# Every third early adapter weight in a place of its own, and two places for a low-rank table

## The chip, the cores and the metric

The kernel runs on one core of one Trainium2 chip. The metric is device time in microseconds (us) of one launch, taken as the median of several runs on the chip. Beside the runs there is one profiled execution, which gives a trace of every instruction with its engine, its start, its length and what it waited for. The engines are TensorE (PE; its weight loads are shown apart as PEld), VectorE (DVE), ScalarE (ACT), GpSimd (POOL) and SyncE (SP). SP computes nothing here; it issues most of the transfers from memory.

## The reference

The input x has 32 samples of 64 rows (H) and 1,024 columns (L), in float32. Four layers each add their output to x:

```python
x = x + L0(x, log_dt, C, log_A_real, A_imag, D, lengths)  # long convolution along L
x = x + einsum('bsi,boi->bso', x, W1[ids1])               # adapter weights, chosen per sample
x = x + einsum('bij,bkj->bik', x, W2[ids2])               # the same with a second set
x = x + gated_ffn(x)                                      # with low-rank parts chosen by ids3
```

Layer 0 builds a kernel of length 1,024 for each of the 64 rows from complex exponentials and convolves each row with it. Layers 1 and 2 multiply each sample (64 x 1024) by a 1024 x 1024 matrix that an index of that sample chooses among 16. Layer 3 is silu(gate) * up, followed by down, with a hidden size of 2,752, and each of gate, up and down has a low-rank part of rank 16, which is chosen per sample too:

```python
t = einsum('bri,bni->bnr', A[ids3], x)
base + einsum('bor,bnr->bno', B[ids3], t) * 0.5
```

## The kernel before, in words

The samples are cut into four chunks (c = 0 to 3) of eight samples, 512 rows in all. The kernel first does the convolution for all 32 samples, then the adapters of chunk 0 alone, and then the gated layers chunk by chunk. The adapters of chunk c + 1 are woven into the gated layers of chunk c, where there is other matmul work around them.

**Adapter weights.** `layers(c)` (line 136) gives the order of the adapters of one chunk: layer 0 of one sample, then layer 1 of the sample before it, and so on, sixteen in all. One adapter's matrix is loaded as eight tiles of 128 x 1024 numbers (KT = 8, 512 KB each); in this document one such tile is a weight. Chunk 0 has 16 x 8 = 128 of them, and they are numbered here in the order of use, from 0. For each weight `adapter` (line 234) does eight matmuls, which the trace shows as sixteen records each, on four column strips side by side, into the PSUM tile pa. After the eighth weight DVE transposes pa into y (L251) and adds y to x (L253). A second layer's adapter waits for the x of its own sample; between the two lies another sample's adapter.

**Places for weights.** `wpool` (line 98) is a ring of nine tiles, named wa in the trace when weights use it. It is shared with all later weights (wf, wr, wd) and with the tiles cv that bring the convolution's results. A tile of the ring is free for a new load when the matmuls that read its last content are done. `early` (lines 125 to 129) is a list of twenty more places: sixteen tiles of a pool `epool` that is closed after the adapters of chunk 0, and four quarters (x_early) of the x tile that later holds chunk 1. They are used once each.

**Order of loads.** The generator `weights` (line 145) issues the loads in the order of use, each with `nc.sync.dma_start` on SP (L161). For each adapter it first reads the matrix index from ids_sb into a register of SP (L151). The line `wt = early.pop(0) if early else wpool.tile(...)` gives the first twenty weights the single-use places and every later one the next tile of the ring. `fetch` (line 171) is called once by each of the sixteen steps of the convolution (`convolve`, line 861), between the load of its input uf (L865) and the loads of its kernels hk (L873): eight weights at the first step and one at each other, 23 in all, kept in the list `ahead`. The rest are issued from `adapter` as the program comes to them. SP works through its instructions in order: a load whose place is not free holds up everything behind it.

**The order on the engines.** The program's text sets the order on TensorE. On the other engines a scheduler of the language sets it, and `tc.issue_after` keeps it from moving an instruction ahead of a given one. The list `loads` holds the last load of each adapter; a read of an index is not moved ahead of the load four adapters back, and the loads of chunk 1's x, of cv and of wd_rest (L188, L193, L549) are not moved ahead of `loads[2 * BC - 1]`, the last weight of chunk 0.

**The low-rank tables.** `b_rows` (line 274) gathers on POOL, with an indirect transfer (L267), the rows of the B tables of gate and up that belong to the samples of the chunk, into a tile bgu of 128 x 4 x 128 numbers (256 KB). It is called once for the part left over (`rest`, m = 10) and for m = 0 to 9 (`gated`). bgu has one buffer (`bufs=1`). `expand` (line 345) multiplies it with tm_g and tm_u into four PSUM tiles pe (L353), which ACT copies to lt (L363). POOL also issues, in its own order, the A tables raw_g, raw_u and raw_d (L297, eight transfers each time) and the gathers into wl (L267); the indices for all gathers come from il, which SP loads (L210) and DVE turns into rowf, rows_half and rows (L212 to L219).

**From the adapters to the gated layers of chunk 0.** After the last weight TensorE does the low-rank products pl_g and pl_u, then `rest`: two pr groups (L470), pe_rest, a third pr group; then the first `gated`: pe from bgu, and seven groups pf (L409) each for gate and up.

Of the kernel before, what the change touches and what calls it, by code (L numbers as in the profile page):

```python
# [8 lines left out]
F32 = mybir.dt.float32  # L9
# [4 lines left out]
SP = mybir.EngineType.SP  # L14
POOL = mybir.EngineType.Pool

P = 128
B, H, L = 32, 64, 1024
NS = 64
KT = L // P  # L20
NCK = 4
BC = B // NCK
# [6 lines left out]
MB = FM // 2  # L29
EARLY = 16  # L30
FIRST_LOADS = 8
PLACES = EARLY + 4 + 9
HA = 4
SEG = 3
TH = TC // 2
# [3 lines left out]
NE = 16  # L39
# [30 lines left out]
def kernel(  # L70
# [23 lines left out]
    nc = tc.nc  # L94

    cpool = ctx.enter_context(tc.tile_pool(name="cpool", bufs=1))
    xpool = ctx.enter_context(tc.tile_pool(name="xpool", bufs=2))
    wpool = ctx.enter_context(tc.tile_pool(name="wpool", bufs=9))
    psum = ctx.enter_context(
        tc.tile_pool(name="psum", bufs=8, space=bass.MemoryType.PSUM)  # L100
    )
# [5 lines left out]
    def ps_tile(name):  # L107
        return psum.tile([P, 512], F32, tag="ps", name=name)
# [8 lines left out]
    def x_tile(c):  # L117
        return xpool.tile([P, KT, TC], F32, tag="x", name=f"x{c}")
# [6 lines left out]
    early = [epool.tile([P, L], F32, tag=f"e{i}", name=f"early{i}") for i in range(EARLY)]  # L125
# [6 lines left out]
    ids_sb = cpool.tile([1, 3 * B], I32, tag="ids", name="ids_sb")  # L132
    nc.sync.dma_start(ids_sb, ids)
    loads = []

    def layers(c):


        for b in range(c * BC, (c + 1) * BC + 1):
            if b < (c + 1) * BC:  # L140
                yield 0, b
            if b > c * BC:
                yield 1, b - 1

    def weights():
        for layer, b in (at_ for c in range(NCK) for at_ in layers(c)):
            with ExitStack() as after:
                if len(loads) > 3:

                    after.enter_context(tc.issue_after(loads[-4]))  # L150
                e = nc.values_load(  # L151
                    ids_sb[0:1, layer * B + b : layer * B + b + 1],
                    engines=[SP],
                    min_val=0,
                    max_val=NE - 1,
                )
            for kt in range(KT):
                name = f"wa{layer}_{b}_{kt}"
                wt = early.pop(0) if early else wpool.tile([P, L], F32, tag="w", name=name)
                w = (w1, w2)[layer]  # L160
                load = nc.sync.dma_start(  # L161
                    wt, w[bass.ds(e, 1), kt].rearrange("e p f -> p (e f)")
                )
                if kt == KT - 1:
                    loads.append(load.ins)
                yield wt

    stream = weights()
    ahead = []

    def fetch(ha):


        for _ in range(FIRST_LOADS if ha == 0 else 1):
            if len(ahead) < PLACES:
                ahead.append(next(stream))

    convolution(tc, cst, consts, xt, xf, ssm, lens, xs[0], cd, ps_tile, fetch)

    came = {}  # L180
    last_add = []

    def bring(c, quarters):

        if quarters[0] == 0:
            xs.append(x_tile(c))
            with tc.issue_after(loads[2 * BC - 1]):
                nc.sync.dma_start(xs[c], xt[:, c])  # L188
        n = H // HA // 4
        for q in quarters:  # L190
            t = wpool.tile([P, n * HA, KT * BC], F32, tag="w", name=f"cv{c}_{q}")
            with tc.issue_after(loads[2 * BC - 1]):
                nc.sync.dma_start(  # L193
                    t.rearrange("p i k -> p (i k)"),
                    cd[c - 1, :, q * n : (q + 1) * n].rearrange("p g e -> p (g e)"),
                )
            came[q] = t
# [36 lines left out]
    def adapter(layer, b):  # L234
        c, lo = b // BC, (b % BC) * H
        acc = ps_tile(f"pa{layer}_{b}")
        for kt in range(KT):
            wt = ahead.pop(0) if ahead else next(stream)
            for s in range(2):
                for i in range(4):  # L240
                    nc.tensor.matmul(  # L241
                        acc[i * S : (i + 1) * S, s * 256 : (s + 1) * 256],
                        xs[c][:, kt, lo + s * S : lo + (s + 1) * S],
                        wt[:, i * 256 : (i + 1) * 256],

                        start=(kt == 0 and s == 0),
                        stop=(kt == KT - 1),
                        skip_group_check=True,
                    )
        y = ypool.tile([P, 512], F32, tag="y", name=f"y{layer}_{b}")  # L250
        nc.vector.transpose(y, acc)  # L251
        cols = xs[c][:, :, lo : lo + H].rearrange("p k (s t) -> p k s t", t=S)
        nc.vector.tensor_add(cols, cols, y.rearrange("p (s k t) -> p k s t", s=2, t=S))  # L253

    def adapters(c):
        for layer, b in layers(c):
            yield adapter(layer, b)

    for _ in adapters(0):
        pass  # L260
    first.close()

    hpool = ctx.enter_context(tc.tile_pool(name="hpool", bufs=1, reuse_waits="tile"))
    gpool = ctx.enter_context(tc.tile_pool(name="gpool", bufs=2, reuse_waits="tile"))

    def gather(t, table, at_):
        nc.gpsimd.indirect_dma_start(  # L267
            out=t,
            out_offset=None,
            in_=table,  # L270
            in_offset=bass.IndirectOffsetOnAxis(ap=at_, axis=0),
        )

    def b_rows(c, piece):
        t = gpool.tile([P, 4, P], F32, tag="bgu", name=f"bgu_{c}_{piece}", bufs=1)
        gather(t.rearrange("p g f -> p (g f)"), bgu, rows[:, c, piece : piece + 1])
        return t

# [115 lines left out]
    def gated(c, m, xb, between):  # L394

        lt = expand(b_rows(c, m), f"{c}_{m}", (("g", 0), ("g", 1), ("u", 2), ("u", 3)))
        lt = lt.rearrange("p (g i) t -> p g i t", g=2)
        cs = []
# [51 lines left out]
    def rest(c):  # L450


        bt = b_rows(c, FM)
        for i in range(3):
            wt = wpool.tile([P, KT, P], F32, tag="w", name=f"wr{i}_{c}")
# [51 lines left out]
    def ffn(c, xb, others):  # L507
# [12 lines left out]
        def between(i):  # L520

            if i < STEPS:
                if c + 1 < NCK:
                    if i in (2, 4):
                        take(c + 1, (i - 2, i - 1))
                    if i in (0, 2):
                        bring(c + 1, (i, i + 1))
            else:
                other(AT_GATED)
# [3 lines left out]
        for block, (m0, m1) in enumerate(BLOCKS):  # L533
            last = m1 == FM
# [6 lines left out]
            if last:  # L541


                wl = gpool.tile([P, 2, 2, L // 2], F32, tag="wl", name=f"wl_{c}", bufs=1)
                for t in (0, 1):
                    wl_t = wl[:, t].rearrange("p i f -> p (i f)")
                    gather(wl_t[FIRST], bd, rows_half[FIRST, c, t : t + 1])
                    with tc.issue_after(loads[2 * BC - 1]):
                        nc.sync.dma_start(wl_t[SECOND], wd_rest)  # L549
                nc.vector.tensor_sub(wl[:, 1, 0], wl[:, 1, 0], wl[:, 1, 1])  # L550
            else:
                ins += [rest1, rest2.rearrange("p i t -> p (i t)")]
# [7 lines left out]
            for h in range(KH):  # L560
                name = f"{c}_{block}_{h}"
# [8 lines left out]
                for s0 in range(m0, m1, SEG):  # L570
# [4 lines left out]
                    at_ = s0 + block  # L575
                    wt = []
                    for i in (0, 1):
                        t = wpool.tile([P, 2, KH, P], F32, tag="w", name=f"wd{i}_{name}_{s0}")
# [4 lines left out]
                    if more:  # L583
                        w = [t[:, 0, nt] for t in wt]
# [3 lines left out]
                    elif end:  # L588
                        w = [[wl[:, t, i, h * P : (h + 1) * P] for i in (0, 1)] for t in (0, 1)]
                        tails = {1: (w[0][0], 0), 3: (w[0][1], 0), 4: (w[1][1], 1), 2: (w[1][0], 1)}  # L590
                    ws = stationary(wt, nt, f"{name}_{s0}")
                    for j in (0, 5, 6, 4, 1, 3, 2):
                        if end and j in tails:
                            w, t = tails[j]
# [44 lines left out]
    for c in range(NCK):  # L639
        xb = ffn(c, xb, adapters(c + 1) if c + 1 < NCK else iter(()))  # L640
# [444 lines left out]
```

## Time and profile before

| what | value |
|---|---|
| median of three runs | 2396.56 us (2396.1 to 2402.57) |
| time of the profiled execution | 2398.25 us |
| span of its trace | 2396.6 us |
| mean granted TensorE clock | 0.998 |
| TensorE busy | 2321.4 us, 97% |
| DVE, ACT, POOL busy | 1098.6, 309.7, 190.2 us |
| convolution on TensorE | to about 193 us |
| adapters of chunk 0 on TensorE | 193.1 to 349.7 us |
| first gated layer's pe | 383.39 us |
| bytes moved | 505.41 MB, mean 211 GB/s |

In the profile's rows of forty slices each digit is the busy share of a slice of about 60 us in tenths, 9 meaning 90% or more. A row of the timeline gives the start and the length in us, the engine, the line, the operation, the tiles (out<-in), the shape and the count of instructions merged into the row, and in brackets the idle time before it with what ended it. A row of waits gives who waited for whom, then the total in us, the number of times and the longest. "SPq" is SP's transfer queue. The clock is the share of full speed that TensorE was granted. The DMA share is the mean busy share of the core's 16 DMA engines.

### The profile page before, as it was taken

What the parts mean: (1) busy time and instruction counts of PE and PEld (TensorE: products, weight loads), DVE (VectorE), ACT (ScalarE), POOL (GpSimd) and SP (SyncE); (2) the same over time, 40 slices, a digit from 0 to 9 for tenths busy, and PEclk for the clock granted to TensorE, in tenths of its full rate; (3) what the DMA queues carried; (4) which work ended last, traced back from release to release, by engine and by line L of the source; (5) the groups of instructions that cost most, each with busy time, mean ns of one, the idle gap of its engine ahead of it and who ended that gap; (6) DMA issues with size and microseconds to landing.
All of it is one profiled execution on the core that took longest, in us unless ns stands there. A gap on an engine that the chain in (4) does not pass through costs nothing. (4 is left out here: it accounts for less than half of the span.)

```text
span 2396.6 us, 46124 instructions
## 1 busy us (share of the span) xinstructions
PE 2321.4 (97%) x19154; PEld 1838.7 (77%) x19154; DVE 1098.6 (46%) x2078; ACT 309.7 (13%) x605; POOL 190.2 (8%) x275
## 2 busy tenths in 40 slices
PE   5999889999999999999999999999999999999999
PEld 5995336877778787877777787777787787888888
DVE  7411124644354534643354544643354544554653
ACT  4200002110011101110011101110011101210210
POOL 4322001000000020000000020000000020000000
PEclk9999999999999999999999999999999999999999
DMA  8997994576666744576666644576666653223311
GB/s 304 367 335 283 408 409 126 185 260 209 237 247 228 245 148 154 185 264 216 240 251 215 241 155 154 180 265 215 242 252 215 239 159 113 82 84 108 100 56 62
DMA packets 165987, 505.41 MB, mean 211 GB/s; under 512 B 20354, under 2 KB 54402, under 8 KB 165266
## 3 DMA queue, kind: packets, MB, share of 16 engines
q1 hardware_dynamic: 147874, 463.87, 55.0%
q0 software_dynamic: 11104, 29.93, 3.8%
q10 hardware_dynamic: 6800, 8.65, 1.0%
q8 instruction: 151, 2.47, 0.4%
q14 instruction: 58, 0.48, 0.1%
HBM read 487.41 MB, written 14.97 MB: 210 GB/s over the span
## 5 line engine op out<-in xcount | busy, mean ns | idle before, releaser
L409 PE MATMUL pf<-xd,wf 128*128 128x256 f32 x2560 | 608.2, 382 | 0.0
L409 PEld LDWEIGHTS pf<-xd,wf 128*128 128x128 f32 x2560 | 482.9, 190 | 74.8 <-issue 6.4
L241 PE MATMUL pa<-wa,x 128*32 128x256 f32 x7872 | 454.9, 381 | 24.5 <-DMA wa<-in_w 21.9
L409 PE MATMUL pf<-xd,s 128*128 128x256 f32 x1920 | 454.0, 379 | 3.9 <-DVE c L430 3.3
L241 PEld LDWEIGHTS pa<-wa,x 128*32 128x32 f32 x7872 | 241.9, 110 | 230.1 <-DMA wa<-in_w 60.8
L409 PEld LDWEIGHTS pf<-xd,s 128*128 128x128 f32 x1920 | 364.6, 190 | 55.0 <-DVE c L430 4.5
L886 PE MATMUL pc<-uf,hk 128*128 128x256 f32 (+7 forms) x1024 | 153.8, 312 | 9.9 <-DMA hk<-kp 6.3
L601 PE MATMUL po<-act,wd 128*128 128x256 f32 x640 | 161.7, 383 | 0.0
L886 PEld LDWEIGHTS pc<-uf,hk 128*128 128x128 f32 x1024 | 148.6, 194 | 14.5 <-issue 8.8
L601 PE MATMUL po<-actd,wd 128*128 128x256 f32 x640 | 159.0, 379 | 0.0
L601 PE MATMUL po<-actd,s 128*128 128x256 f32 x640 | 159.0, 379 | 0.0
L267 POOL DMA_INDIRECT bgu<-in_bgu,rows x44 | 46.0, 1045 | 1363.2 <-PE pe L353 1292.6
L434 DVE TENSOR_TENSOR c<-pf,u 128x256 f32<-128x256 f32 x80 | 34.0, 425 | 235.5 <-PE pf L409 235.5
L601 PEld LDWEIGHTS po<-act,wd 128*128 128x128 f32 x640 | 119.5, 190 | 22.9 <-issue 6.3
L601 PEld LDWEIGHTS po<-actd,wd 128*128 128x128 f32 x640 | 121.6, 190 | 16.5
L601 PEld LDWEIGHTS po<-actd,s 128*128 128x128 f32 x640 | 121.6, 190 | 16.5
L363 ACT COPY lt<-pe 128x512 f32<-128x512 f32 x160 | 82.2, 600 | 341.1 <-PE pe L353 254.6
L251 DVE STREAM_TRANSPOSE y<-pa 128x512 f32<-128x512 f32 x64 | 45.5, 710 | 134.1 <-PE pa L241 134.1
L438 DVE TENSOR_TENSOR c<-c,lt 128x1024 f32<-128x1024 f32 x80 | 97.9, 1224 | 5.1
L381 DVE TENSOR_TENSOR s<-wf 128x512 f32<-128x512 f32 x80 | 54.9, 687 | 86.1 <-DMA wf<-in_wg 46.3
L381 DVE TENSOR_TENSOR s<-wd 128x384 f32<-128x384 f32 x64 | 31.2, 488 | 134.9 <-PE po L601 86.8
L470 PE MATMUL pr<-x,wr 128*128 128x512 f32 x192 | 84.2, 595 | 0.0
(169 smaller groups left out, 1828.0 us busy)
## 6 DMA issues: line engine op xcount, KB each, us to landing
wa<-in_w SPq DMA_DIRECT2D x492, 512.0 KB, 7.5
wf<-in_wg SPq DMA_DIRECT2D x80, 512.0 KB, 4.1
wf<-in_wu SPq DMA_DIRECT2D x80, 512.0 KB, 3.8
wd<-in_wd SPq DMA_DIRECT2D x96, 384.0 KB, 4.7
hk<-kp SPq DMA_DIRECT2D x30, 1024.0 KB, 8.3
x<-in_xt SPq DMA_DIRECT2D x4, 2048.0 KB, 11.1
uf<-in_xf SPq DMA_DIRECT2D x16, 512.0 KB, 5.1
early<-in_w SPq DMA_DIRECT2D x16, 512.0 KB, 8.5
```

The lines of the kernel that those rows point to most:

```text
L241: nc.tensor.matmul(acc[i * S : (i + 1) * S, s * 256 : (s + 1) * 256], xs[c][:, kt, lo + s * S : lo + (s + 1) * S], wt[:, i * 256 : (i + 1) ...
L251: nc.vector.transpose(y, acc)
L267: nc.gpsimd.indirect_dma_start(out=t, out_offset=None, in_=table, in_offset=bass.IndirectOffsetOnAxis(ap=at_, axis=0),)
L363: nc.scalar.copy(lt[:, :n, 2 * H * j : 2 * H * (j + 1)], ps[:, : n * 2 * H].rearrange("p (i t) -> p i t", i=n),)
L381: nc.vector.tensor_add(s1, a21, a22)
L409: nc.tensor.matmul(ps, ws[j][:, kt, :], xb[j][:, kt, :], start=start and kt == 0, stop=kt == KH - 1, skip_group_check=True,)
L434: nc.vector.tensor_add(cq[:, 1], pb, u)
L438: done = nc.vector.tensor_add(cf, cf, lt[:, g].rearrange("p i t -> p (i t)"))
L470: nc.tensor.matmul(ps, wt[:, kt, :], xs[c][:, kt, :], start=(kt == 0), stop=(kt == KT - 1),)
L601: nc.tensor.matmul(pss[j], ws[j][:, i, :], ab[m - m0][j], start=(m == m0 and home[j] % 2 == 0), stop=(m == m1 - 1), skip_group_check=True,)
L886: nc.tensor.matmul(ps[:, j, d * B :], hk[:, j, d * P : (d + 1) * P], uf[:, i + j, : KT - d, :].rearrange("p k b -> p (k b)"), start=(d == ...
```

## The change

The first 60 weights are now shared out between the two kinds of place by their number. Every third one (2, 5, 8, ..., 59) has one of the twenty single-use places, and the other forty go through the ring of nine. A new generator `first_weights` issues what can be issued without any wait, in the order of use: the nine first rotating weights (0, 1, 3, 4, 6, 7, 9, 10, 12) and all twenty with an own place, 29 in all. `fetch` draws from it, and what is left is issued right after the convolution. `weights` then hands out the weights in the order of use: those that are held already, and the others with a load at that point. The index of a matrix is read once for the part of an adapter that is issued early and once more for the part that is issued later. `done_first` takes the place of `loads[2 * BC - 1]`; both are the last load of chunk 0.

Apart from that, bgu takes the pool's own number of buffers, which is two.

```diff
+    def load_weight(e, layer, b, kt, own):
+        name = f"wa{layer}_{b}_{kt}"
+        wt = early.pop(0) if own else wpool.tile([P, L], F32, tag="w", name=name)
+        w = (w1, w2)[layer]
+        load = nc.sync.dma_start(wt, w[bass.ds(e, 1), kt].rearrange("e p f -> p (e f)"))
+        return wt, load.ins
+
+    own = {3 * i + 2 for i in range(len(early))}
+    held = {}
+
+    def first_weights():
+        rotating = [k for k in range(3 * len(early)) if k not in own][:ROTATING]
+        last, at_ = [], None
+        for k in sorted([*own, *rotating]):
+            layer, b = list(layers(0))[k // KT]
+            if at_ != k // KT:
+                at_, e = k // KT, adapter_id(layer, b, last)
+                last.append(None)
+            held[k], last[-1] = load_weight(e, layer, b, k % KT, k in own)
+            yield
+
     def weights():
+        k = 0
         for layer, b in (at_ for c in range(NCK) for at_ in layers(c)):
...
             for kt in range(KT):
-                wt = early.pop(0) if early else wpool.tile([P, L], F32, tag="w", name=name)
...
+                if k in held:
+                    yield held.pop(k)
+                else:
+                    if e is None:
+                        e = adapter_id(layer, b, loads)
+                        loads.append(None)
+                    wt, loads[-1] = load_weight(e, layer, b, kt, False)
+                    yield wt
+                k += 1
...
         for _ in range(FIRST_LOADS if ha == 0 else 1):
-            if len(ahead) < PLACES:
-                ahead.append(next(stream))
+            next(before, None)

     convolution(tc, cst, consts, xt, xf, ssm, lens, xs[0], cd, ps_tile, fetch)
+    for _ in before:
+        pass
...
-            wt = ahead.pop(0) if ahead else next(stream)
+            wt = next(stream)
...
-        t = gpool.tile([P, 4, P], F32, tag="bgu", name=f"bgu_{c}_{piece}", bufs=1)
+        t = gpool.tile([P, 4, P], F32, tag="bgu", name=f"bgu_{c}_{piece}")
```

## The prediction

> **What bounds the kernel now.** I read the page's slices first, then one-stretch tables, the waits of SP's DMA queue, and the timeline of TensorE at the two places that the diff touches.
>
> ```profile
> PE   5999889999999999999999999999999999999999
> DMA  8997994576666744576666644576666653223311
> ```
>
> TensorE fills every slice from the eighth on, so time can only be won or lost in the first 400 us, where its 75 us of idle time (2396.6 - 2321.4) nearly all lie: 28 us in the first 60 us, a few in the convolution, some 23 between 215 and 350, 5 at 378. Later it waits about 4 us. The stretches of the first adapters (columns: stretch, length, then busy us and count of PE, PEld, DVE, ACT, POOL; then clock, DMA share, GB/s):
>
> ```profile
> 195.00:200.00 5.00, 5.00 (x96) 3.03 (x100) 0.00 (x0) 0.00 (x0) 4.17 (x8) 1.00 0.37 121
> 200.00:205.00 5.00, 5.00 (x100) 3.01 (x96) 1.41 (x2) 0.00 (x0) 2.00 (x4) 1.00 0.23 70
> 205.00:210.00 5.00, 5.00 (x100) 2.99 (x92) 1.41 (x2) 1.05 (x1) 2.99 (x4) 1.00 0.21 62
> 225.00:349.00 124.00, 101.00 (x1512) 40.39 (x1516) 15.50 (x22) 1.99 (x2) 0.00 (x0) 1.00 1.03 408
> ```
>
> From 195 to 212 TensorE is full and the DMA engines are nearly idle; from 225 to 349 it is the reverse: transfers at 408 GB/s, TensorE waiting for each weight. The stage is bound by transfers, and it wastes 17 us of them at its start. The SP queue (210 us window from 200; columns: total, times, longest us) says why:
>
> ```profile
> SPq L161 <- PE pa L241: 28.1, 9, 25.8
> ```
>
> One wait of 25.8 us: the 30th load stands at SP until TensorE has used the 21st weight, since the first twenty lie in places that are used once. TensorE's timeline (start, us, instructions, count, idle before):
>
> ```profile
> 208.31 3.64 PE L241 MATMUL pa<-x_early,x 128*32 128x256 f32 x64
> 211.76 10.62 PE L241 MATMUL pa<-wa,x 128*32 128x256 f32 x192
> 223.24 1.07 PE L241 MATMUL pa<-wa,x 128*32 128x256 f32 x16 [0.86 <-DVE y L251]
> 225.72 2.18 PE L241 MATMUL pa<-wa,x 128*32 128x256 f32 x32 [1.42 <-DMA wa<-in_w]
> ```
>
> A weight is 16 records; 192 in 10.62 us is 0.885 us a weight when none is waited for. Weight 33 (from 0) starts at 225.72 and the last ends at 349.69: 95 weights at 1.305 us, the price by transfer. The issue of the first rotating load after the gap is at 212.87.
>
> The second place is at 378:
>
> ```profile
> 378.35 1.19 POOL L267 DMA_INDIRECT bgu<-in_bgu,rows  x1 [2.87 <-issue]
> 383.39 1.24 PE L353 MATMUL pe<-tm_g,bgu 32*128 32x128 f32 x16 [4.96 <-DMA bgu<-in_bgu,rows]
> 385.41 3.77 PE L409 MATMUL pf<-xd,wf 128*128 128x256 f32 x8
> ```
>
> TensorE stands 4.96 us for a gather that POOL issued behind sixteen raw_d loads, and then runs slowly: eight pf matmuls take 3.77 us, where the same eight take 1.89 at 402.8. The clock over this stretch:
>
> ```profile
> 384.00:386.00 2.00, 2.00 (x30) 1.68 (x27) 0.71 (x2) 0.53 (x2) 0.16 (x1) 0.50 0.00 0
> 386.00:388.00 2.00, 2.00 (x6) 1.64 (x5) 0.00 (x0) 1.52 (x4) 0.82 (x1) 0.50 0.13 27
> 390.00:392.00 2.00, 2.00 (x11) 1.77 (x10) 0.43 (x1) 0.37 (x1) 0.00 (x0) 1.00 0.00 0
> ```
>
> Half clock until about 389.
>
> **What the Trainium skill says.** "TensorE: Matmul & The Clock Gate", part 1, says that an idle window of about 3.4 us halves TensorE's clock and that as long a busy stretch restores it. The trace agrees for the 4.96 us gap (about 5.5 us at half), and is harsher once: after a 1.99 us gap at 131 the clock was 0.50 from 133.2 to 136; gaps of 1.50 and 1.42 us cost nothing. "DMA: Bandwidth & Descriptors", section "Anatomy of one DMA", gives a fixed 2.0 us plus bytes over 436 GB/s, 3.2 us for 512 KB; the quickest weight here landed 3.3 us after issue. The same page, "Issuing engines are not separate DMA queues": POOL's and SP's transfers share the 16 engines. The trace agrees: at 215 to 220 raw_u and weights together moved only 294 GB/s at a share of 0.92.
>
> **Part 1, the places.** Every third of weights 0 to 59 gets one of the twenty single-use places; weights 0, 1, 3, 4, 6, 7, 9, 10, 12 fill the ring of nine. As before 29 weights are loaded ahead, 23 of them inside the convolution and six behind it, none waiting for TensorE. Bytes and matmuls are the same; only which place a weight lies in changes.
>
> Weight 13 now needs the place of weight 0, which TensorE has used at about 195.6, so its load issues at about 195.8 and not at 212.87: 17.1 us of transfer time gained. What comes off:
> - The idle DMA time was not quite empty. POOL's raw_g, bgu and wl gathers and the last cd write ran in it: 0.37, 0.23 and 0.21 of three 5 us stretches, 4.05 us, less weights that were still arriving at 195. They now share the engines with weights. With the second bgu table (256 KB, about 0.65 us at 408 GB/s) I take 4.4 us; bounds 3.1 (1.25 MB at 408 GB/s) and 6.5 (small packets twice as dear, as raw_u's were: the first 33 weights came 4.4 us later than 1.305 us each and a 3.5 us landing give).
> - Pacing. While own places last, three weights on TensorE (2.66 us) free two places (2.61 us of transfer): balanced. 31 loads lose 31 x 0.02, 0.7 us.
>
> Net 17.1 - 4.4 - 0.7 = 12.0 us. From the other end: 195.8 + 3.5 + 98 x 1.305 + 1.07 (last weight) + 4.4 (raw_u, as before) + 4.4 + 0.7 = 337.8, against 349.7; the same sum without the two new terms from 212.87 gives 349.7, as measured. After 350 the work is TensorE's, so an earlier start comes off the end.
>
> The lead of nine rotating places is about 12 us of TensorE's work, and a lone landing takes 3.5, so TensorE has no reason to stop in weights 0 to 59.
>
> **Queues.** In the built order SP has three more reads of ids inside the convolution (0.27 + 0.15 + 0.02 us each; the interval from uf to the weight's issue is 1.15 us with one and 0.55 without). They stand ahead of the hk loads, for which TensorE waits there already (gaps of 0.32, 1.50, 1.99). Bounds: 0 if SP waits for a place anyway, 1.8 if all shows; a longer gap may add a half clock of 1.6. I take 0.8. Behind the convolution il's load moves behind six weights: I estimate that it lands before 195; on DVE rowf and rows then stand ahead of the first y transpose, needed at 201.65, 6 us of cover. Without that cover the second layer's first adapter would come late by the excess.
> On POOL the first wl gather moves behind raw_u, and both wl gathers now wait for TensorE's use of weight 17 (early5, about 211); their reader on DVE is at 378, so 160 us hide it. The raw_u loads, needed at 353, stand ahead of them.
>
> **Part 2, the second bgu place.** The gather for m = 0 of the first chunk moves from behind raw_d to before raw_u, near 208. TensorE goes from pr straight to pe: the 4.96 us go, and with them the half clock. The distance from this pe to the next is 383.39 to 411.55, 28.16 us; undisturbed it is 1.10 + 24.37 = 25.47 (pe and pf at 2195 in the chain); the difference is 2.69 us. Sum 7.65. What is late next: the pe banks come free with lt_rest at 373, wf's sums are done at 377.5, ACT's two rest operations end at 380.6 ahead of the lt copies, and the second half's sums at 384.7, wanted at about 391. DVE loses its 6.6 us of slack there, so I leave 0.6 us for a wait on it (0.92 occurs one step later now). Net 7.0. Bounds: 2 if something else takes most of the gap, 7.7. In the later chunks bgu's gathers move ahead of raw_g or raw_u, but wait for the same pe as the gather that stood there before; TensorE waits 0.2 us for bgu after 400, so nothing is gained or lost.
>
> **Sum.** -12.0 - 7.0 + 0.8 = -18.2 us. The profiled span is 2396.6 (that execution's time 2398.25), the median 2396.56; both stand alike, so I predict 2378. Under 0.3% (7 us) a difference could not be told from none; the parts' bounds give -21.7 (-14.0 - 7.7) to -8.5 (-9.9 - 2.0 + 3.4).
>
> **Rivals.**
> - *Only the places pay* (0.14): the gap at 378 is kept by DVE or ACT, which run close behind there. For it: DVE works from 377.4 to 384.7 without a pause. Against: TensorE needs its results only at 391. 2396.6 - 12 + 0.8 - 1 = 2384.
> - *Only bgu pays* (0.13): the transfers are not brought forward, because a load of the ring waits at SP's head, or POOL's small packets eat the idle time. For it: 6.5 us is the upper bound of sharing and SP is one queue. Against: each load waits only for weights long used. 2396.6 - 7 + 0.8 - 2 = 2388.
> - *The change does not do what it says* (0.03): bgu waits and the 25.8 us wait both remain. 2396.
> - *Slower* (0.04): in the adapters' stage TensorE waits in gaps of 2 us or more instead of 0.2 us crumbs, and each halves the clock, as at 131. At 1.6 to 2.7 us a drop, one per adapter of the chunk (16 x 2.2, 35 us) gives 2378 + 35 = 2413; it decides from twelve drops on. Against: the 1.42 us gap at 224 dropped nothing, and transfers come steadily.
> - *Both parts as forecast* takes 0.66.
>
> **How the numbers follow.** Forecast alone: 2373 to 2383. With the two one-part rivals the range of eight in ten is 2372 to 2390: below, the better bound (2375) less half the scatter of the three runs (6.5 us); above, the second rival. Faster by over 0.3% (below 2389.4): 0.66 + 0.14 + 0.08 of the third = 0.88; slower by over 0.3%: 0.04; the rest 0.08.
>
> **What would show it.** SP's longest wait for pa falls from 25.8 us to under 5; DMA is above 300 GB/s from about 197; the last pa matmul ends near 338; the bgu wait at the first pe is gone and the clock stays 1.00 there. It is wrong if pa ends at 345 or later, if a gap of over 2 us opens in the convolution or the adapters, or if pe still waits.

## The result, and the profile after

The changed kernel takes 2379.77 us (median of five runs, 2377.0 to 2384.88), against 2396.56 us (five runs, 2392.81 to 2402.57): a ratio of 0.9931, 95% interval 0.991 to 0.9953. Repeated in a later set of runs it took 2381.35 against 2399.23, a ratio of 0.9927 (0.9915 to 0.994). The forecast was 2378, between 2372 and 2390. The profiled execution after has a span of 2375.4 us against 2396.6; it is the quickest of its five, so its 21.2 us are more than the medians' 16.8.

The same rows of the page after, TensorE and DMA by slice:

```profile
PE   5999889999999999999999999999999999999999
DMA  8999994666766654666766654566766653223311
```

The fourth DMA digit, the slice that holds the gap, has gone from 7 to 9. The stretches of the adapters of the changed kernel (columns as before: stretch, length, busy us and count of PE, PEld, DVE, ACT, POOL, then clock, DMA share, GB/s):

```profile
195.00:200.00 5.00, 5.00 (x100) 2.99 (x92) 1.06 (x6) 0.00 (x0) 3.90 (x7) 1.00 0.80 237
200.00:205.00 5.00, 5.00 (x99) 2.99 (x92) 1.41 (x2) 0.00 (x0) 1.63 (x4) 1.00 1.03 395
205.00:210.00 5.00, 5.00 (x100) 3.01 (x96) 1.41 (x2) 0.91 (x1) 2.02 (x2) 1.00 1.03 392
240.00:336.00 96.00, 81.13 (x1256) 35.93 (x1248) 13.71 (x20) 1.99 (x2) 0.00 (x0) 1.00 1.03 408
```

TensorE is as full as before from 195 to 210, and the DMA engines, at a share of 0.23 and 0.21 before, are now at 1.03. SP's waits of the changed kernel for the adapters' matmuls (185 to 340 us; columns: total, times, longest):

```profile
SPq L161 <- PE pa L269: 22.2, 25, 7.9
```

25.8 us at a stretch have become 7.9, and those lie at the end of the convolution: SP has issued everything that needs no freed place by 185, and the first place is free only when TensorE has used weight 0. After that no such wait is longer than 1.2 us. SP's first load behind the wait, before and then after:

```profile
212.87 46.44 SPq L161 DMA_DIRECT2D wa<-in_w  x38
194.90 3.99 SPq L161 DMA_DIRECT2D wa<-in_w  x4
```

TensorE before, at the first and the last pa and at the second pe of the gated layer:

```profile
193.13 0.64 PE L241 MATMUL pa<-early,x 128*32 128x256 f32 x8
...
348.62 1.07 PE L241 MATMUL pa<-wa,x 128*32 128x256 f32 x16 [0.20 <-DMA wa<-in_w]
...
411.55 0.73 PE L353 MATMUL pe<-tm_g,bgu 32*128 32x128 f32 x16
```

TensorE after, at the same places and at the first gated layer's pe:

```profile
192.43 0.64 PE L269 MATMUL pa<-wa,x 128*32 128x256 f32 x8
...
336.17 1.07 PE L269 MATMUL pa<-wa,x 128*32 128x256 f32 x16 [0.20 <-DMA wa<-in_w]
...
365.90 0.73 PE L382 MATMUL pe<-tm_g,bgu 32*128 32x128 f32 x16
366.45 0.62 PE L382 MATMUL pe<-tm_u,bgu 32*128 32x128 f32 x16
367.01 1.99 PE L438 MATMUL pf<-xd,wf 128*128 128x256 f32 x8
...
391.38 0.73 PE L382 MATMUL pe<-tm_g,bgu 32*128 32x128 f32 x16
```

pa ends at 337.24, not 349.69. The row of pe has no wait in brackets, its matmuls take 0.73 us and not 1.24, and the first eight pf 1.99 and not 3.77.

Where the 21.2 us between the two traces lie:

| stretch | before | after | difference |
|---|---|---|---|
| start to the first pa (convolution) | 193.13 | 192.43 | -0.70 |
| first pa to the end of the last pa | 156.56 | 144.81 | -11.75 |
| end of pa to the first gated layer's pe | 33.70 | 28.66 | -5.04 |
| that pe to the next | 28.16 | 25.48 | -2.68 |
| next pe to the end | 1985.05 | 1984.02 | -1.03 |

The last row is no gain that can be told from chance: in the profiles of the other kernels below that stretch takes 1983.2 to 1985.5 us, with the change or without.

### The profile page after: what moved, and what is told of

Its sections match the earlier page's. It is cut to its first block, busy times and chain, and to the rows that moved or that the text cites. A ratio compares the mean times of both kernels' runs of the same rounds, so it can differ in the third digit from the quotient of the medians.

```text
span 2375.4 us, 46146 instructions
## 1 busy us (share of the span) xinstructions
PE 2311.7 (97%) x19154; PEld 1839.0 (77%) x19154; DVE 1098.0 (46%) x2078; ACT 309.6 (13%) x605; POOL 190.3 (8%) x275
## 4 chain that ended last, share of the span: by engine, by line
PE 90%; DMA 7%; DVE 2%; issue 1%; ACT 0%; SPq 0%; POOL 0%; DVEq 0%; ACTq 0%
PE pf L438 40%; PE po L630 21%; PE pa L269 16%; PE pc L915 4%; DMA wa<-in_w 4%; PE pr L499 4%; PE po L625 2%; PE pe L382 2%; DMA hk<-kp 1%; PE pl_d L354 1%; DVE x L232 0%; DMA wf<-in_wg 0%; DVE br L717 0%; PE pl_u L354 0%; PE pl_g L354 0%
## 5 line engine op out<-in xcount | busy, mean ns | idle before, releaser
L269 PE MATMUL pa<-wa,x 128*32 128x256 f32 x7872 | 453.4, 380 | 19.2 <-DMA wa<-in_w 17.1
```

The costliest lines, as they stand in the source:

```text
L269: nc.tensor.matmul(acc[i * S : (i + 1) * S, s * 256 : (s + 1) * 256], xs[c][:, kt, lo + s * S : lo + (s + 1) * S], wt[:, i * 256 : (i + 1) ...
```

## Experiments

**Each part alone.** The places without the second buffer, and the second buffer without the places:

```diff
# e1_places_only: the changed kernel, with
+        t = gpool.tile([P, 4, P], F32, tag="bgu", name=f"bgu_{c}_{piece}", bufs=1)
# e2_bgu_only: the kernel before, with
+        t = gpool.tile([P, 4, P], F32, tag="bgu", name=f"bgu_{c}_{piece}")
```

> The new places alone, bgu with one buffer as before. Theory (two separate gains): the last pa matmul ends at 337 as in the changed kernel, the first gated layer's pe still waits about 5 us for its gather and runs into half clock, so about 28.2 us lie between it and the next pe; time 12 to 13 us under before, 2384. Rival (one gain: the gather was late only because the adapters ended late and POOL's queue with them): the wait at pe is under 2 us and the time is 2378 to 2381.

> Two bgu buffers alone, places as before. Theory: pa ends at 349 to 350, the wait at the first pe and the half clock behind it are gone (25.5 us to the next pe), time 7 to 8 us under before, 2389. Rival (DVE or ACT, close behind there, keep the gap): a wait of 2 us or more at pe or in the first pf groups, time 2392 to 2395.

Places alone: 2387.3 us against 2399.6, ratio 0.9955 (0.9938 to 0.9972). Two bgu buffers alone: 2393.5, ratio 0.9975 (0.9965 to 0.9986). The two together make 0.45% + 0.25% = 0.70%, where the change has 0.69%; with intervals of 0.1 to 0.2% to either side, so close an agreement is in part chance. In microseconds the places gain 12.3, as expected, and the buffer 6.1, a little less than the 7 to 8 expected; its median, 2393.5, taken by itself lies in the rival's 2392 to 2395, but the kernel before was 3 us slower in this set, and the trace decides. TensorE at the first two pe, with the places alone:

```profile
371.64 0.92 PE L382 MATMUL pe<-tm_g,bgu 32*128 32x128 f32 x16 [4.67 <-DMA bgu<-in_bgu,rows]
398.74 0.73 PE L382 MATMUL pe<-tm_g,bgu 32*128 32x128 f32 x16
```

and with the buffer alone:

```profile
379.26 0.73 PE L353 MATMUL pe<-tm_g,bgu 32*128 32x128 f32 x16
404.74 0.73 PE L353 MATMUL pe<-tm_g,bgu 32*128 32x128 f32 x16
```

With the places alone the stage of the adapters is 144.12 us, the wait of 4.67 us is still there, and 27.10 us lie between the two pe. With the buffer alone the stage is 157.80 us, the wait is gone and 25.48 us lie between them. So the parts are two gains in two places, and neither needs the other. The rival that the gather was late only because the adapters ended late is out, and so, by the trace, is the one by which DVE or ACT keep the gap.

**The half clock by itself.** The kernel before, with twenty spare matmuls in the gap. Their result is not used, and the gather comes as late as it did:

```diff
+        bt = b_rows(c, m)
+        if c == 0 and m == 0:
+            fill = ps_tile("fill")[:, :TH]
+            for i in range(20):
+                nc.tensor.matmul(
+                    fill, xs[0][:, 0, :P], xs[0][:, 0, :TH], start=True, stop=True
+                )
-        lt = expand(b_rows(c, m), ...)
+        lt = expand(bt, ...)
```

> The kernel before with twenty spare matmuls (128x256, results unused) on TensorE ahead of the first gated layer's pe, where it stands still for 4.96 us; the gather is as late as before. Theory (TensorE runs at half clock behind the gap because it stood still): the clock stays at 1.00 and 25.5 us lie between this pe and the next instead of 28.2, though pe starts no earlier; 2 to 3 us in all. Rival (the slow matmuls behind the gap have another cause, such as tiles that come late): still 28 us.

TensorE in that kernel (start, us):

```profile
378.37 8.80 PE L400 MATMUL fill<-x 128*128 128x256 f32 x40
387.10 0.73 PE L353 MATMUL pe<-tm_g,bgu 32*128 32x128 f32 x16
...
412.57 0.73 PE L353 MATMUL pe<-tm_g,bgu 32*128 32x128 f32 x16
```

The filling took longer than the gap, so pe starts 3.7 us later than before; yet the next pe is at 412.57, 25.47 us on. The clock was 1.00 throughout. That leaves the standstill as the cause of the slow matmuls behind it, and 2.7 us as its price in the kernel before: the gap of 4.96 us cost 7.6 us. The price is not the same each time. Behind the gap of 4.67 us with the places alone it was 1.6 us (27.10 - 25.47), and behind one of 4.83 us in the kernel before without tables (below) 2.3 us (27.74 - 25.47).

**How the own places are spread.** Every second of the first forty weights, or every fourth of the first eighty, in place of every third of sixty:

```diff
-    own = {3 * i + 2 for i in range(len(early))}
+    own = {2 * i + 1 for i in range(len(early))}   # e3_every_second
+    own = {4 * i + 3 for i in range(len(early))}   # e4_every_fourth
```

(and the 3 in `rotating` likewise)

> As the changed kernel, but every second of the first forty weights has the place of its own. Theory (while own places last, TensorE frees a rotating place every 1.77 us where a transfer takes 1.3): eleven loads come at TensorE's pace and lose 0.47 us each, so pa ends about 5 us later, at 342. Rival (only the start of the transfers matters, not how the own places are spread): pa ends at 337.

> As the changed kernel, but every fourth of the first eighty weights has the place of its own. Theory (transfers are the bound from the first freed place on, TensorE's waits only move forward): pa ends within 1 us of the changed kernel, 336 to 338. Rival (the place for every third fits TensorE's pace, and waits that come earlier are not made up): pa ends 2 us later or more, 339 to 342, with TensorE waiting in the first 60 weights.

The place at which pa ends shifts with the start of the stage, which differs from run to run (below), so I compare the length of the stage: 144.8 us for every third, 147.1 for every second (192.81 to 339.94), 144.8 for every fourth (197.01 to 341.78). This is not the measure that I had named: by its end alone, 341.8, every fourth would fall to its rival (339 to 342), and it is the late start, 197.0 against 192.4, that makes up for it. By the length it behaves as the theory says. Every second is worse, but by 2.3 us and not by 5. That is a miss, and a question: is the loss by pace smaller, or does something fill the time that it leaves?

**POOL's tables.** The 1 MB of A tables for gate and up that POOL loads in this stage for chunk 0, left out of three kernels, which have zeros in their place:

```diff
+        if c == 0 and n == KT:
+            nc.gpsimd.memset(raw, 0.0)
-        for b in range(BC):
+        for b in range(BC) if c or n != KT else ():
```

> The changed kernel without the A tables of gate and up of chunk 0 (raw_g and raw_u, 1 MB together): zeros are written in their place, so the low-rank parts of gate and up of that chunk are left out. Theory (POOL's tables share the 16 engines with the weights, and the stage is bound by transfers): the adapters' stage, first to last pa, is 2.6 us (1 MB at 408 GB/s) to 5 us shorter than the changed kernel's 144.8. Rival (the tables fall into slack): under 1 us shorter.

> The kernel before without the same A tables of chunk 0 (zeros in their place, the low-rank parts of gate and up of that chunk left out). Theory: here raw_g fell into the idle transfer time and cost nothing, and only raw_u meets weights, so the stage shortens by 1.3 to 3 us from 156.6, that is by 1 to 2.5 us less than in the changed kernel; that difference is what sharing takes off the change's gain. Rival: the same shortening in both.

> Every second weight in a place of its own, and the A tables of gate and up of chunk 0 left out (zeros in their place, so the low-rank parts of gate and up of that chunk are left out). Theory (spreading the places too tightly leaves transfer time that POOL's tables fill, so that they cost nothing there and the 5 us expected for every second shrank to 2.3): without tables the stage stays near 147, 5 us over the 141.5 of every third without tables. Rival (the loss by pace is 2.3 us by itself): the stage is 143 to 144.5.

| own places | stage with the tables | without | tables cost |
|---|---|---|---|
| the first twenty weights (before) | 156.56 | 153.87 | 2.7 |
| every third (after) | 144.81 | 141.47 | 3.3 |
| every second | 147.13 | 146.17 | 1.0 |

Each of these is one profile, and the stage differs by 1 to 2 us between profiles of kernels that have the same places (155.6 to 157.8 us with those of before, 144.1 to 145.7 with every third). With every second weight the loss by pace is 4.7 us (146.17 - 141.47), as expected and well above that scatter. The tables fill the transfer time that the pace leaves open, and so most of the loss did not show: from 208 to 218 the transfers of that kernel run at 344 and 379 GB/s with the tables, and at 273 and 314 without. The second question stays open. The tables' share in what comes off the change's gain is 0.6 us by these figures (3.3 - 2.7), where I had expected 1 to 2.5; but 0.6 is within the scatter, so that neither the expected share nor the rival, the same cost in both kernels, is excluded.

**The reads of ids.** One read for each early weight, and all reads ahead of the first weight:

```diff
# e8_read_each
-            if at_ != k // KT:
-                at_, e = k // KT, adapter_id(layer, b, last)
-                last.append(None)
+            at_, e = k // KT, adapter_id(layer, b, last)
+            last.append(None)
# e11_reads_first, before the loop over the weights
+        ids_first = {}
+        for k in sorted([*own, *rotating]):
+            layer, b = list(layers(0))[k // KT]
+            if k // KT not in ids_first:
+                ids_first[k // KT] = adapter_id(layer, b, [])
```

> The changed kernel with a read of ids for every early weight and not for every adapter: one in each of the sixteen steps of the convolution, where the changed kernel has one in six of them. Theory of the prediction (a read delays the hk loads, and TensorE waits for these): ten more reads at 0.6 us put the first pa 1 to 6 us later than 192.4. Rival (the reads are hidden, since transfers and not SP's issue set the pace of the convolution): the first pa within 1 us, or within what it differs by between runs.

> The changed kernel once more, beside the next two on one chip: 2377 to 2385, ratio to before 0.991 to 0.995.

> The changed kernel with all eight reads of ids ahead of the first weight's load, so that none stands in the convolution's later steps. Theory (each read there puts the hk loads 0.6 us later and TensorE waits for them): the first pa 1 to 3 us earlier than in the changed kernel and the median 1 to 3 us lower. Rival (the pace of the convolution is that of the transfers): the same median within the runs' scatter of 4 us, and the ends of the convolution scatter as in the other runs.

With ten reads more in the later steps (and seven more in the first, where eight weights are loaded), the first pa was at 198.3. That is inside the 1 to 6 us that the theory gave, but a kernel with the same loads and reads in its convolution as the changed one (the one without tables) had it at 202.5, and others at 192.4 to 197.0, so this run decides nothing. With no read in the later steps it was at 196.0 and the median 2382.53, beside 195.9 and 2381.35 for the changed kernel itself in the same set: the 1 to 3 us that the theory promised did not come. No cost of the reads can be seen; one of less than 1 us, as the prediction had it, would be lost in the scatter.

**What makes the convolution scatter.** TensorE's gaps in the convolution from 100 us on, in that second trace of the changed kernel:

```profile
113.01 4.76 PE L915 MATMUL pc<-uf,hk 128*128 128x256 f32 x32 [1.86 <-DMA hk<-kp]
135.22 6.41 PE L915 MATMUL pc<-uf,hk 128*128 128x256 f32 x32 [2.88 <-issue]
157.23 18.56 PE L915 MATMUL pc<-uf,hk 128*128 128x256 f32 x128 [1.02 <-DVE tmp L709]
177.41 18.56 PE L915 MATMUL pc<-uf,hk 128*128 128x256 f32 x128 [1.62 <-issue]
```

Each is a gap between two steps, and behind the one of 2.88 us thirty-two matmuls take 6.41 us instead of 4.76: half clock again. In each step the early weight stands on SP ahead of the two hk loads. Moving it, with its read, between the two:

```diff
             nc.sync.dma_start(uf, xf[:, ha : ha + HA])
-            fetch(ha)
+            if ha == 0:
+                fetch(ha)
...
                 if i:
                     between()
+                elif ha:
+                    fetch(ha)
```

> The changed kernel with each early weight behind the first of its step's two hk loads, not ahead of both (the first step as it is). Theory (in the convolution TensorE's gaps of 1 to 2.7 us are waits for hk behind a weight in the same queue, and those over 2 us bring half clock): hk lands about 1.8 us earlier (1.3 of transfer and 0.5 of issue), the gaps at 110 to 180 fall below 1 us, the first pa is at 187 to 191, and the time is 3 to 6 us under the changed kernel. Rival (the transfers are full there, so a weight only moves its delay to the next hk): the gaps stay in sum, time within 2 us of the changed kernel.

2372.51 us (2371.96 to 2373.18), against 2399.23 for the kernel before, ratio 0.9886 (0.9872 to 0.99), and 2381.35 for the changed kernel in the same set. It beats both. TensorE's waits from 60 to 200 us in that kernel:

```profile
PE pa L269 <- POOL x L933: 1.1, 1, 1.1
PE pc L918 <- DMA hk<-kp: 0.6, 2, 0.4
```

In the changed kernel the same list reads

```profile
PE pc L915 <- issue: 3.3, 3, 1.8
PE pc L915 <- DMA hk<-kp: 1.9, 3, 1.4
PE pc L915 <- DVE tmp L709: 1.5, 1, 1.5
PE pa L269 <- POOL x L930: 1.1, 1, 1.1
```

The 6.7 us of waits for the next step are down to 0.6, the first pa is at 185.7, and the four times of the kernel (its profile's included) lie within 1.2 us where those of the changed kernel lie within 5 to 8. So most of the changed kernel's scatter sat in these gaps and in the half clock that some of them bring; for the kernel before, whose times lie within 6 to 10 us, the same was not tried. The rival, that a weight only passes its delay on to the next hk, is out. That it is the weight and not the read rests on the run with all reads first, which gained nothing. The gain, 8.8 us, is above the 3 to 6 that I expected, mainly because the changed kernel's convolution ended at 195.9 in the profile of this set and not at the 192.4 from which I counted; the first pa came 10.2 us earlier, and some 2 us of this were lost again behind it (the stage of the adapters is 145.7 us here, against 144.6).

## Why the prediction was right, point by point

The median fell by 16.8 us, 17.9 in the later set, and the profile by 21.2, where the prediction had 18.2. Its two main terms each held, by the traces and by the kernels with one part alone. That the median came within 2 us of 2378 is luck as well: single times of the changed kernel lie up to 8 us apart.

- **The bound.** That the adapters' stage is bound by transfers and wastes them while the twenty single-use places are used up: shown. Leaving out 1 MB of transfers shortens the stage in both kernels. The first load after the gap issues 2.5 us after the first pa (194.90) and no longer 19.7 us after it (212.87), a gain of 17.3 us where the prediction had 17.1. Spreading the places by four gives the same stage as by three, as it must where transfers are the bound.
- **The signs.** SP's longest wait was to fall under 5 us and is 7.9. The sign was badly chosen, not the theory: by the prediction's own times SP has nothing to issue between the last early load, at about 185, and the use of weight 0, near 195. A gap of over 2 us in the convolution was to show the forecast wrong. The first trace has none; the second trace of the changed kernel has one of 2.88 us, but so has the kernel with the filled gap, whose places are those of before, with 2.36 us, so nothing points to the change as its cause.
- **What comes off.** The stage got 11.75 us shorter; predicted 12.0. So 5.5 us came off, against 4.4 + 0.7. The total held; how it is made up is not shown. The A tables' part, 0.6 us by the two kernels without them, is within the scatter. The rest was not measured by itself: the second bgu table, the first wl gather and the start of the rotating loads are left for it. The prediction's check "from the other end" is weaker than it looks: of the 4.4 us for raw_u the trace gives 4.1 by weight 33 (225.72 - 212.87 - 3.5 - 4 x 1.305), and the rest is what makes the sum meet 349.7.
- **TensorE has no reason to stop in the first 60 weights.** Not quite: it waited four times there, at 218.6 to 229.8, 0.2 to 1.5 us each, while raw_u and wl were landing. Every fourth weight has the same stage, so I take it that these waits cost nothing further.
- **The reads of ids, 0.8 us.** This step is not borne out. The kernel with all reads first was no quicker; the first pa came 0.7 us earlier in one trace of the changed kernel and 2.8 us later in the other, so a term of this size can't be read from either. The prediction also gave TensorE's gaps there to SP's issue of hk with a read before it; what stands before hk and matters is a weight of 512 KB in the same queue.
- **il and wl.** Both covered, as said: no wait for rows or wl shows on TensorE or DVE's first transpose. il came at 195.6, slightly later than estimated, with DVE idle for 2.35 us before it and the first transpose at 200.94. The wl gathers issue at 220.3 and 221.6, 144 us ahead of their reader at 365.5.
- **The second bgu place.** 5.04 + 2.68 = 7.7 us; predicted 7.0, with 0.6 taken off for a new wait on DVE. That wait did not come: the first gated layer runs without a gap. The half clock as the cause of the slow matmuls behind the gap was argued in the prediction and is now shown by the filled gap.
- **After that.** 1.0 us more came off later in this pair of profiles, where I had nothing. It is within the scatter: the kernel with the weight behind the first hk has the change too and takes 1985.07 us there, as before.
- **The slower rival**, a gap of 2 us or more in each adapter, did not occur: in the first trace the longest wait in the stage is 1.7 us and the clock stays at 1.00. The half clock itself did come there once, in the second trace of the changed kernel: after a wait of 1.76 us the clock was 0.50 from 270 to 272. Yet that stage took 144.6 us, no longer than the 144.8 of the first trace. So a drop in a stage bound by transfers need not cost the 1.6 to 2.7 us at which the rival priced it.

"TensorE: Matmul & The Clock Gate" of the Trainium skill (part 1) says that the window in which activity is judged runs freely. That fits the last section, where the length of a gap alone does not decide, but no run here shows where such a window lies.

## What to carry to other kernels

When a stage is bound by transfers, look for the stretch in which it isn't: buffers that are used once and stand at the front of the order let the compute engine run on while no transfer can start, and mixing them with rotating ones moves the same loads forward. A gap on TensorE of some microseconds is worth more than its length, because of the half clock behind it (here 1.6 to 2.7 us on gaps of 4.7 to 5.0). And in a queue that is full, put the load that is waited for next ahead of one that has time: that was worth 8.8 us here, between the 6.1 of the second buffer and the 12.3 of the places.

## What the runs showed of the hardware

The prediction took a gap of 1.99 us as enough for half clock, from one case. Over the traces, from 60 us on, the length of a gap alone does not decide it. Of fifteen gaps of 1.99 to 2.88 us in the convolution nine were followed by slow matmuls (1.99, 2.08, 2.10, 2.36, 2.45, 2.48, 2.52, 2.68 and 2.88) and six were not (2.25, 2.33, 2.34, 2.36, 2.69 and 2.72), one of 2.36 us on each side; shorter ones, of up to 1.97 us, never were. In the adapters' stage, where shorter waits lie around them, it took less: after five gaps of 1.67 to 2.10 us the clock fell (1.67, 1.75, 1.76, 1.99 and 2.10), after four of 1.74 to 2.53 it did not (1.74, 1.76, 2.18 and 2.53). After the three of 4.67 to 4.96 us it always fell. What decides in between is not shown; nearly all of these gaps are shorter than the 3.4 us that the prediction quotes. For example, in the kernel with every second weight and in that with every fourth:

```profile
113.09 4.76 PE L915 MATMUL pc<-uf,hk 128*128 128x256 f32 x32 [2.69 <-DMA hk<-kp]
```

```profile
115.09 6.41 PE L915 MATMUL pc<-uf,hk 128*128 128x256 f32 x32 [2.52 <-DMA hk<-kp]
```

The longer gap left the clock alone and the shorter one halved it, which cost 1.65 us (6.41 - 4.76).
